# Sorted tokens of a mixture of experts: results added to x by accumulating indexed transfers, weights carried in the sorted rows

## The chip, the core and the metric

The kernel runs on one core of one Trainium2 chip. Its time is the device time of one execution in microseconds (us). The engines of the core work side by side, each through its own list of instructions: TensorE (PE in the profile, with its weight loads as PEld), VectorE (DVE), ScalarE (ACT), GpSimd (POOL), and SyncE (SP), which only issues transfers here. Transfers with an index per row (indexed transfers) are issued by GpSimd.

## The reference

The input x holds 8 batches of 1024 tokens of 128 numbers, in float32. Three layers follow one another:

```python
x = x + 0.5 * ffn(layernorm(x))     # layer 0
x = x + attention(layernorm(x))     # causal, one head, with rotary embedding
x = x + 0.5 * ffn(layernorm(x))     # layer 1, the same weights
```

The ffn is a mixture of 16 experts. A token's scores are `sigmoid(t @ gate_w.T)`; the four experts with the highest biased scores are chosen, and their scores, scaled to the sum 2.5, are the token's weights. An expert computes `silu(t @ g) * (t @ u)` with 64 units and multiplies by its down matrix. A shared expert is added for every token.

```python
for e in experts:
    y = y + weight[:, e] * (h_e(t) @ w2[e].T)     # weight is 0 for experts not chosen
y = y + h_shared(t) @ w2_shared.T
```

## The kernel before

A tile is 128 tokens, a group is 4 tiles (512 tokens), and a batch has 2 groups. Layer 0 of all batches and layer 1 of batches 4 to 7 are computed *dense*: every expert for every token. The experts are taken two at a time, in 8 pairs (class `Group`): a gate product (L651) and an up product (L657) of 512 columns on TensorE, the activation on ScalarE (L664), their product on VectorE (L668, "the units of a pair"), the weighing by the tokens' weights on GpSimd or VectorE (L673), and the down product (L684) that sums over pairs in PSUM. The weights are written to memory and spread from there over the partitions (L588, L597). One result per group is added to x on VectorE (L694) and, in layer 1, stored (L698).

Layer 1 of batches 0 to 3 is *sorted* (classes `SortedGroup`, `Chunk`, `Rows`), in two chunks of two batches. The router picks four experts per token. The chunk computes for each of its 16 tiles and each choice k the row at which the token stands when tokens are ordered by expert (`place`). The normalized tokens are scattered to these rows in memory by 64 indexed transfers of 128 rows (L1017). Blocks of 8 tiles of sorted rows are then loaded, transposed, and multiplied by the matrices of the expert that owns each tile (L1106, L1116, L1136); the results are copied from PSUM, one half of the block by ScalarE and the other by VectorE (L1143), and stored in `results`. At the end each tile of tokens gathers its four rows back, one indexed transfer for each k (L838). Meanwhile x with the shared expert's part has been kept in memory (`keep`, L817) and its buffer given back; it is fetched again (L834), VectorE adds each gathered row times its weight (L847), and the tile is stored (L854). The weight for each choice is looked up by three VectorE operations per group (L1003, L1009, L1013).

Attention (classes `Heads`, `Query`) lies between the layers, batch by batch.

The order of instructions on each engine is written by a planner when the program is built (class `Plan`). Every step has an engine, an assumed duration, a rank, the buffers that it takes and frees, and the steps that it waits for. The planner repeatedly picks the step that can begin first, and of those the one of lowest rank. A weighing may go to GpSimd or to VectorE, whichever can begin first (`instead`). After two indexed transfers in a row it puts a dummy operation of GpSimd, the pause (L247). So a change of a few steps can change the order of everything, and on the chip each engine keeps to the order as it was written.

Of the kernel before, what the change touches and what calls it, by code (L numbers as in the profile page):

```python
# [27 lines left out]
class Step:  # L28


    def __init__(self, engine, work, rank, emit, take, free, table, moves, indexed=False):
# [7 lines left out]
        self.left, self.next, self.ready, self.end = 0, [], 0.0, None  # L39


class Plan:
# [10 lines left out]
    def __init__(self, begin, pause):  # L53
        self.pause = pause
        self.in_row = 0
        self.steps = []
        self.places = {}
        self.held = {}
        self.free_at = dict.fromkeys(self.ENGINES, begin)
        self.transfers = begin  # L60
        self.table = None
# [9 lines left out]
    def add(self, engine, work, rank, emit, after=(), take=(), free=(), table=None, moves=0,  # L71
# [9 lines left out]
        return s  # L81

# [23 lines left out]
    def begin_of(self, s, t):  # L106
        t = max(t, s.ready)
        for pool in s.pools:
# [21 lines left out]
    def run(self):  # L130
# [12 lines left out]
        while todo:  # L143
# [29 lines left out]
            s.emit()  # L173
            todo -= 1
# [18 lines left out]
def kernel(  # L193
# [33 lines left out]
    LEAD = 8  # L227
# [25 lines left out]
    for name, n in {"gu": 3, "y": 1, "short": 3, "score": 2, "xs": 2}.items():  # L253
        plan.pool(name, n)
    buffers = {}
    for name, n, shape in (
        ("x", 9, [P, GT, D]),
        ("xn", 3, [P, GT, D]),
        ("xnc", CB * NG + 1, [P, GT, D]),
# [21 lines left out]
        ("combc", 1, [P, CT, E]),  # L281
        ("at", 1, [P, CT, E]),
        ("eq", 1, [P, GT, TOPK, E]),
        ("row", 4, [P, GT, D]),
        ("wt", 4, [P, GT, 2 * D]),
        ("got", 4, [P, TOPK + 1, D]),
        ("hs", 2, [P, W]),
    ):
        if not SORTED and name in ("xnc", "hTs", "chosen", "combc", "at", "eq", "row", "wt", "hs", "got"):
# [162 lines left out]
    def norm_steps(key, b, g, rank, after, tag, uses):  # L452
# [10 lines left out]
        def scale(j):  # L463
            nc.vector.tensor_scalar(
                buf(tag, n)[:, j, :], x_of(b, g)[:, j, :], mvs[n][:, j, 0:1], rstd[:, j : j + 1],
# [8 lines left out]
    def turn_steps(n, rank, after, tag, out_tag, uses):  # L474
# [3 lines left out]
        def turn():  # L478
            for j in range(GT):
                nc.tensor.transpose(tiles_of(bank_of(a))[:, j, :], buf(tag, n)[:, j, :], ident)  # L480
# [5 lines left out]
        return act(0.6, rank, copy, after=[s], free=end_short(a))  # L486
# [3 lines left out]
    class Group:  # L490
# [111 lines left out]
        def spread_steps(self, rank, after):  # L602
# [7 lines left out]
            return [  # L610
                sp(
                    1.0, rank, lambda h=h: self.load_weights(h), after=[s],
                    take=[("cb", (n, h), NP // 2)], moves=1.0,
                )
                for h in range(2)
            ]
# [86 lines left out]
        def expert_steps(self, p, last, hT, weights, shared):  # L703
# [5 lines left out]
            ready = []  # L709
            for k in range(NP):  # L710
# [3 lines left out]
                    0.86, rank, lambda k=k: self.gate(k), after=[hT, have_gate[w]],  # L714
                    take=[("pair", a, 1), ("gu", a, 1), ("sg", a, 1), ("hid", a, len(self.parts))],
                    free=[("hT", n)],
                )
                u = pe(
# [12 lines left out]
                ready.append(s)  # L731
            ends = []
# [31 lines left out]
        def steps(self, p, last, after):  # L764
# [4 lines left out]
            hT = turn_steps(n, rank, [s], "xn", "hT", 2 * NP + 2)  # L769
            shared = self.shared_steps(rank + 0.5, [hT])  # L770
            s = self.route_steps(rank, [hT])
            weights = self.spread_steps(rank, [s])
            return self.expert_steps(p, last, hT, weights, shared)
# [754 lines left out]
```

## Time and profile before

| | |
|---|---|
| median of 3 runs | 958.57 us (958.16 to 962.21) |
| profiled execution, own time | 960.61 us |
| its span, first to last instruction | 958.9 us |
| mean granted TensorE clock | 0.984 of full speed |
| instructions | 16331 |
| transfers | 136.93 MB, mean 143 GB/s |

The profile's page comes from one execution. "Busy" is the time in which an engine has an instruction at work. The slices cut the span into 40 parts of 24 us; each digit is the busy share in tenths. A group row names a line of the kernel, engine and operation, what it writes and reads with the shape, the count, then the busy time in us and the mean of one in ns, and then the idle time of the engine before them and what ended it. A timeline row gives the start in us, the duration in us, and the same names; a bracket at its end gives the idle time before it and the instruction that released it. In the trace a product of 512 columns is two matmul records[...].

### The profile page before, as it was taken

How to read it: one execution, taken by the hardware profiler on the slowest of the kernel's cores; microseconds unless marked ns; L12 is line 12 of the kernel's file. 1: busy time of each engine (PE TensorE's matmuls, PEld its weight loads, DVE VectorE, ACT ScalarE, POOL GpSimd, SP SyncE). 2: the span in 40 equal slices, each digit the busy share in tenths (PEclk: the TensorE clock that was granted, in tenths of full speed). 3: DMA queues.
4: the chain of work that ended last, by engine and by line, in shares of the span. 5: the costliest groups of instructions: out<-in, count | busy, mean ns of one | idle time of the engine just before them, and what ended most of it. 6: DMA issues, size and time to landing. Idle time of an engine off the chain costs nothing. (4 is left out here: it accounts for less than half of the span.)

```text
span 958.9 us, 16331 instructions
## 1 busy us (share of the span) xinstructions
PE 910.9 (95%) x5226; PEld 629.4 (66%) x5226; DVE 792.0 (83%) x2297; ACT 487.1 (51%) x818; POOL 657.3 (69%) x614
## 2 busy tenths in 40 slices
PE   9899999999998698999999999999999899999995
PEld 5556676666665475766676686776767766656663
DVE  7899878978888989889999866778888987777864
ACT  6336646558555324565565754566557464333220
POOL 2464615514488778988388988837877867888786
PEclk9899999999999899999999999999999999999998
DMA  5866327423132543134436887877598766566572
GB/s 167 201 181 175 77 69 209 119 49 89 45 110 57 126 122 88 50 82 110 117 104 179 219 215 212 228 189 196 147 254 196 197 192 147 136 159 145 135 170 53
DMA packets 147862, 136.93 MB, mean 143 GB/s; under 512 B 12160, under 2 KB 117440, under 8 KB 147648
## 3 DMA queue, kind: packets, MB, share of 16 engines
q1 hardware_dynamic: 138304, 117.83, 48.8%
q0 software_dynamic: 8192, 16.79, 6.3%
q10 hardware_dynamic: 1280, 1.26, 0.4%
q8 instruction: 41, 0.67, 0.3%
q14 instruction: 45, 0.37, 0.1%
HBM read 99.40 MB, written 36.44 MB: 142 GB/s over the span
## 5 line engine op out<-in xcount | busy, mean ns | idle before, releaser
L673 POOL TENSOR_TENSOR hid<-hid,cb 128x512 f32<-128x512 f32 x144 | 182.5, 1278 | 138.0 <-DVE hid L668 121.1
L684 PEld LDWEIGHTS psum<-wd,hid 128*128 128x128 f32 x1536 | 192.2, 195 | 34.2 <-issue 27.5
L684 PE MATMUL psum<-wd,hid 128*128 128x128 f32 x1536 | 202.9, 280 | 1.8 <-POOL hid L673 1.8
L657 PE MATMUL psum<-hT,wu 128*128 128x512 f32 x384 | 197.2, 595 | 3.5 <-DVE hid L668 3.5
L651 PE MATMUL psum<-hT,wg 128*128 128x512 f32 x384 | 198.2, 598 | 0.0
L664 ACT ACTIVATE sg<-psum 128x512 f32<-128x512 f32 x192 | 113.9, 598 | 156.9 <-PE psum L651 128.0
L668 DVE TENSOR_TENSOR hid<-psum,sg 128x512 f32<-128x512 f32 x192 | 131.2, 687 | 50.0 <-PE psum L657 33.1
L1017 POOL DMA_INDIRECT rows<-xnc,place x128 | 130.0, 1016 | 38.6 <-issue 29.5
L838 POOL DMA_INDIRECT got<-results,place x128 | 129.7, 1013 | 29.6 <-issue 28.3
L657 PEld LDWEIGHTS psum<-hT,wu 128*128 128x128 f32 x384 | 73.0, 191 | 96.9 <-issue 84.1
L1369 PEld LDWEIGHTS psum<-v,prT 128*128 128x128 f32 x576 | 71.0, 192 | 18.1 <-issue 13.1
L247 POOL TENSOR_TENSOR spare<-spare 128x4 f32<-128x4 f32 x76 | 80.5, 1060 | 1.7
L847 DVE SCALAR_TENSOR_TENSOR got<-got,wk 128x128 f32<-128x128 f32 x128 | 67.8, 544 | 14.3 <-DMA got<-results,place 13.3
L651 PEld LDWEIGHTS psum<-hT,wg 128*128 128x128 f32 x384 | 62.1, 192 | 25.4 <-issue 23.6
L1369 PE MATMUL psum<-v,prT 128*128 128x128 f32 x576 | 73.8, 276 | 1.8 <-ACT prT L1360 1.4
L1329 PE MATMUL psum<-k,q 128*128 128x512 f32 (+2 forms) x192 | 71.7, 497 | 2.6 <-DVE hid L668 2.4
L461 POOL TENSOR_TENSOR rs_f<-rs_f,neg_half 128x4 f32<-128x4 f32 x32 | 34.9, 1090 | 47.4 <-DVE rs_f L458 46.7
L443 DVE BATCH_NORM_STATS2 st<-x 128x6 f32<-128x128 f32 x192 | 53.4, 278 | 5.1 <-DMA x<-in_x 3.2
L1342 ACT ACTIVATE pr<-psum,top 128x128 f32<-128x128 f32 (+3 forms) x64 | 47.2, 740 | 17.5 <-DVE top L1339 12.5
L664 ACT ACT_TABLE_LOAD x38 | 48.8, 1283 | 8.3 <-PE psum L651 7.1
L1329 PEld LDWEIGHTS psum<-k,q 128*128 128x128 f32 x192 | 32.0, 195 | 28.3 <-issue 21.0
L1338 DVE TENSOR_REDUCE top<-psum 128x1 f32<-128x128 f32 (+3 forms) x64 | 48.4, 757 | 2.0
(143 smaller groups left out, 1505.2 us busy)
## 6 DMA issues: line engine op xcount, KB each, us to landing
cb<-cd SPq DMA_DIRECT2D x96, 512.0 KB
wt<-in_w_table SPq DMA_DIRECT2D x160, 128.0 KB
rows<-sums SPq DMA_DIRECT2D x20, 512.0 KB
row<-rows SPq DMA_DIRECT2D x40, 256.0 KB
results<-row SPq DMA_DIRECT2D x40, 256.0 KB
x<-in_x SPq DMA_DIRECT2D x16, 256.0 KB
kept<-x SPq DMA_DIRECT2D x8, 256.0 KB
rows<-xnc,place POOLq DMA_INDIRECT x128
```

What stands on the lines that cost most here:

```text
L247: nc.gpsimd.tensor_tensor(spare, spare, spare, ALU.pow)
L651: nc.tensor.matmul(pair_of(("gu", self.id, k))[0], wg[:, k * P : (k + 1) * P], self.hT(), start=True, stop=True,)
L657: nc.tensor.matmul(pair_of(("gu", self.id, k))[1], wu[:, k * P : (k + 1) * P], self.hT(), start=True, stop=True,)
L664: nc.scalar.activation(buf("sg", a), pair_of(a)[0], AF.Silu)
L668: nc.vector.tensor_tensor(buf("hid", a), pair_of(a)[1], buf("sg", a), ALU.mult)
L673: engine.tensor_tensor(hid, hid, cb, ALU.mult)
L684: nc.tensor.matmul(y[:, cols], units[:, cols], wsd if k == NP else wd[:, k, :], start=(self.terms[part] == 1 and j == tiles[0]), stop=(sel ...
L838: nc.gpsimd.indirect_dma_start(out=buf("got", (self.id, j))[:, k, :], out_offset=None, in_=self.chunk.results, in_offset=bass.IndirectOffs ...
L847: nc.vector.scalar_tensor_tensor(got[:, TOPK, :], got[:, k, :], self.chunk.weight[:, self.n * GT + j, k : k + 1], got[:, TOPK, :], ALU.mul ...
L1017: nc.gpsimd.indirect_dma_start(out=self.views[t * TOPK + k], out_offset=bass.IndirectOffsetOnAxis(ap=self.place[:, t, k : k + 1], axis=0), ...
L1329: nc.tensor.matmul(s[:, c:e], q[:, i * P : self.width], k[:, c:e], start=True, stop=True)
L1369: nc.tensor.matmul(o, buf("prT", self.id)[:, j, :], buf("v", self.b)[:, j, :], start=(j == 0), stop=(j == i),)
```

## The change

- The normalized tokens of a sorted group get 16 more columns, which hold the token's weights for the 16 experts, already halved (`R = D + E`, buffers `xnc`, rows in memory, loaded rows). They travel with the token in the scatter.
- After a block of sorted rows is loaded, VectorE finds each row's weight: it compares the owner of the row's tile (`own`) with the experts' numbers, multiplies by the 16 carried weights, and sums (`Rows.weights`). The results are multiplied by that weight as they leave PSUM (`result`): on ScalarE in four scalings of 128 columns, on VectorE in one product of 512.
- A gather adds its rows directly to x in SBUF (`compute_op=ALU.add`). The four additions of one tile wait for one another. They are ranked by k first, then by tile. After the last one the whole group is stored from x in one transfer.
- The lookup of weights per choice, the copy of x in memory, its fetch, VectorE's weighted addition, and the store by tiles are gone.
- x now stays in its buffer from loading until it is stored; there are 12 such buffers in place of 9.
- The planner gets `line`: a group's gate products and weight loads enter in the order in which groups were transposed. The gates of a group follow one another, as do its two weight loads, which also wait for the shared expert's step. The transposes of the second half of a query wait for those of the first.

```diff
--- before.py
+++ after.py
+    def line(self, name, key, enter, first, last):
+        self.lines[name] = []
+        enter.enters = (*enter.enters, (name, key))
+        for s in (first, last):
+            s.heads = name, key
+        last.leaves = True
...
         t = max(t, s.ready)
+        if s.heads and self.lines[s.heads[0]][:1] != [s.heads[1]]:
+            return float("inf")
...
             s.emit()
+            for name, key in s.enters:
+                self.lines[name].append(key)
+            if s.leaves:
+                self.lines[s.heads[0]].pop(0)
...
+    R = D + E
+    LEAD = 9
     SW = P // GT
...
-        ("x", 9, [P, GT, D]),
+        ("x", 12, [P, GT, D]),
         ("xn", 3, [P, GT, D]),
-        ("xnc", CB * NG + 1, [P, GT, D]),
+        ("xnc", CB * NG + 1, [P, GT, R]),
...
-        ("combc", 1, [P, CT, E]),
         ("at", 1, [P, CT, E]),
-        ("eq", 1, [P, GT, TOPK, E]),
-        ("row", 4, [P, GT, D]),
+        ("above", 1, [P, E, CT]),
+        ("row", 4, [P, GT, R]),
+        ("own", 2, [P, NS]),
+        ("part", 2, [P, GT, E]),
         ("wt", 4, [P, GT, 2 * D]),
-        ("got", 4, [P, TOPK + 1, D]),
         ("hs", 2, [P, W]),
     ):
...
+            loads = []
+            for h in range(2):
+                s = sp(
+                    1.0, rank, lambda h=h: self.load_weights(h), after=[s, shared],
                     take=[("cb", (n, h), NP // 2)], moves=1.0,
                 )
-                for h in range(2)
-            ]
...
-                    0.86, rank, lambda k=k: self.gate(k), after=[hT, have_gate[w]],
+                    0.86, rank, lambda k=k: self.gate(k),
+                    after=[hT, have_gate[w], *gates[-1:]],
                     take=[("pair", a, 1), ("gu", a, 1), ("sg", a, 1), ("hid", a, len(self.parts))],
                     free=[("hT", n)],
                 )
...
+            plan.line("gates", n, turned, gates[2], gates[-1])
...
-                buf("combc", self.chunk.n, "chunk")[:, self.tiles, :], self.sel, 0.5 * ROUTE_SCALE,
+                buf("xnc", self.id)[:, :, D:], self.sel, 0.5 * ROUTE_SCALE,
...
-        def keep(self):
-            nc.sync.dma_start(out=self.kept, in_=x_of(self.b, self.g))
...
-            s = dve(0.69, rank, self.shared_add, after=[s, normed], free=end_short(a))
-            self.away = sp(
-                0.5, rank, self.keep, after=[s], free=[("x", (self.b, self.g))], moves=0.25
-            )
+            self.summed = dve(0.69, rank, self.shared_add, after=[s, normed], free=end_short(a))
             return self.route_steps(rank, [hT])
-        def fetch(self, j):
-            nc.sync.dma_start(out=buf("got", (self.id, j))[:, TOPK, :], in_=self.kept[:, j, :])
         def gather(self, j, k):
             nc.gpsimd.indirect_dma_start(
-                out=buf("got", (self.id, j))[:, k, :], out_offset=None, in_=self.chunk.results,
+                out=x_of(self.b, self.g)[:, j, :], out_offset=None, in_=self.chunk.results,
                 in_offset=bass.IndirectOffsetOnAxis(
                     ap=self.chunk.place[:, self.n * GT + j, k : k + 1], axis=0
                 ),
-            )
-        def gathered(self, j, k):
-            got = buf("got", (self.id, j))
-            nc.vector.scalar_tensor_tensor(
-                got[:, TOPK, :], got[:, k, :], self.chunk.weight[:, self.n * GT + j, k : k + 1],
-                got[:, TOPK, :], ALU.mult, ALU.add,
-            )
-        def store_sorted(self, j):
-            t = self.g * GT + j
+                compute_op=ALU.add,
+            )
+        def store_sorted(self):
             nc.sync.dma_start(
-                out=in_tiles(out, self.b, slice(t, t + 1)),
-                in_=buf("got", (self.id, j))[:, TOPK : TOPK + 1, :],
+                out=in_tiles(out, self.b, tiles_of_group(self.g)), in_=x_of(self.b, self.g)
             )
         def gather_steps(self, rank, after):
+            ends = []
             for j in range(GT):
-                a = (self.id, j)
-                r = rank + 0.02 * j
-                before = [
-                    sp(
-                        0.5, r, lambda j=j: self.fetch(j), after=[*after, self.away],
-                        take=[("got", a, 1)], moves=0.064,
+                s = self.summed
+                for k in range(TOPK):
+                    s = pool(
+                        1.24, rank + k + 0.02 * (self.n * GT + j),
+                        lambda j=j, k=k: self.gather(j, k), after=[s, *after],
+                        moves=0.064, indexed=True,
                     )
-                ]
-                for k in range(TOPK):
-                    got = [
-                        pool(
-                            1.24, r, lambda j=j, k=k: self.gather(j, k),
-                            after=before if k == 0 else [*after, first], moves=0.064, indexed=True,
-                        )
-                    ]
-                    first = got[0] if k == 0 else first
-                    before = [
-                        dve(
-                            0.44, r, lambda j=j, k=k: self.gathered(j, k), after=[*got, *before]
-                        )
-                    ]
-                sp(
-                    0.5, r, lambda j=j: self.store_sorted(j), after=before, free=[("got", a)],
-                    moves=0.064,
-                )
+                ends.append(s)
+            sp(
+                0.5, rank, self.store_sorted, after=ends, free=[("x", (self.b, self.g))],
+                moves=0.25,
+            )
...
-            self.rows = dram.tile([NS * P, D], F32, name=f"rows{n}")
+            self.rows = dram.tile([NS * P, R], F32, name=f"rows{n}")
...
-        def weights(self, m, part):
...
+        def belongs(self):
+            nc.vector.tensor_copy(buf("own", self.n), bank_of(("op", self.n))[:, :NS])
...
+        def weights(self, h):
+            part = buf("part", (self.id, h))
+            q = 2 * self.i + h
+            shape = [P, GT, E]
+            nc.vector.tensor_tensor(
+                part, buf("own", self.chunk.n)[:, q * GT : (q + 1) * GT].unsqueeze(2).broadcast_to(shape),
+                counts[:, :E].unsqueeze(1).broadcast_to(shape), ALU.is_equal,
+            )
+            nc.vector.tensor_tensor(part, part, buf("row", (self.id, h))[:, :, D:], ALU.mult)
+            nc.vector.tensor_reduce(self.weight[h], part, AX.X, ALU.add)
         def result(self, h):
-            (nc.scalar.copy, nc.vector.tensor_copy)[h](
-                buf("row", ("y", self.id, h)), tiles_of(bank_of(("xd", self.id, h)))
-            )
+            y = tiles_of(bank_of(("xd", self.id, h)))
+            out = buf("row", ("y", self.id, h))
+            if h == 0:
+                for j in range(GT):
+                    nc.scalar.mul(out[:, j, :D], y[:, j, :], self.weight[h][:, j : j + 1])
+            else:
+                nc.vector.tensor_tensor(
+                    out[:, :, :D], y, self.weight[h].unsqueeze(2).broadcast_to([P, GT, D]), ALU.mult
+                )
...
+                weighed.append(
+                    dve(
+                        0.6, rank, lambda h=h: self.weights(h), after=[s, own],
+                        take=[("part", a, 1)],
+                        free=[("row", a), ("xs", a), ("part", a), ("own", self.chunk.n)],
+                    )
                 )
...
-                    (0.59, 0.69)[h], UNITS, lambda h=h: self.result(h), after=[s], free=end_short(b),
+                    (1.04, 0.69)[h], UNITS, lambda h=h: self.result(h), after=[s, weighed[h]], free=end_short(b),
...
```

## The prediction

> **What bounds the kernel now.** I read the page's shares and slices first, to see which engine is full and when.
>
> ```profile
> PE 910.9 (95%) x5226; PEld 629.4 (66%) x5226; DVE 792.0 (83%) x2297; ACT 487.1 (51%) x818; POOL 657.3 (69%) x614
> ...
> PE   9899999999998698999999999999999899999995
> ...
> DVE  7899878978888989889999866778888987777864
> ...
> POOL 2464615514488778988388988837877867888786
> ```
>
> TensorE is full nearly everywhere, so only what makes TensorE wait is worth time. VectorE is nearly as full in the first half; GpSimd fills up in the second.
>
> How much TensorE loses I took from the chain of waits and the timeline. Where it never waits a 512-column product takes 0.86 us, four 128-column products 0.89, four transposes 0.44. At these prices all its instructions sum to 876.8 us. Against that sum, its transposes of normalized tokens (L480) give a clock: one stands at 281.4 in the sum and at 304.1 in the trace (22.6 lost), others at 316.5 and 356.7 (40), 469.1 and 522.3 (53), 807.8 and 878.5 (71). TensorE ends at 949.7: 72.8 us lost, 54 of them before position 495, about 19 after.
>
> Why the first half loses I asked of VectorE's instructions, in their order, each at its mean from the groups. At the mark "units n done" (L668) the VectorE sum is ahead of TensorE's by 24.5 us at 281, 41.9 at 374, 50.1 at 459 and 51.8 at 492, close to the losses above; after that it falls to 7.5. So up to about 495 VectorE sets the pace. The timeline shows the sharpest case:
>
> ```profile
> 322.47 8.59 POOL L673 TENSOR_TENSOR hid<-hid,cb 128x512 f32<-128x512 f32 x7
> ...
> 323.62 7.52 DVE L790 TENSOR_TENSOR chosen<-rp,bi 128x64 f32<-128x64 f32 x1
> ...
> 332.55 0.45 PE L512 MATMUL psum<-ident,lt 128*128 128x128 f32 x1 [5.41 <-DVE x L1377]
> ```
>
> A small VectorE operation with two SBUF inputs (shortest of its line: 0.215 us) lasts as long as GpSimd's seven weighings in a row; TensorE then waits 5.4 us. Last, the tail:
>
> ```profile
> 949.05 0.61 PE L684 MATMUL psum<-wsd,sh 128*128 128x128 f32 x4
> 949.70 0.42 DVE L694 SCALAR_TENSOR_TENSOR x<-psum,x 128x256 f32<-128x256 f32 x1 [0.34 <-PE psum L684]
> ...
> 950.15 0.38 SPq L698 DMA_DIRECT2D out_x<-x  x1
> ...
> 953.30 1.01 POOL L838 DMA_INDIRECT got<-results,place  x1 [0.19 <-issue]
> ...
> 956.01 0.35 DVE L847 SCALAR_TENSOR_TENSOR got<-got,wk 128x128 f32<-128x128 f32 x1 [1.89 <-DMA got<-results,place]
> 956.39 0.33 SPq L854 DMA_DIRECT2D out_x<-got  x1
> ```
>
> TensorE is done at 949.7; gathers of the last tile, their additions and a store of 64 KB hold the end to 958.9.
>
> **The change, part by part.** Prices come from these rows (the last three stand for operations that the trace does not have):
>
> ```profile
> L673 POOL TENSOR_TENSOR hid<-hid,cb 128x512 f32<-128x512 f32 x144 | 182.5, 1278 | 138.0 <-DVE hid L668 121.1
> ...
> L838 POOL DMA_INDIRECT got<-results,place x128 | 129.7, 1013 | 29.6 <-issue 28.3
> ...
> L247 POOL TENSOR_TENSOR spare<-spare 128x4 f32<-128x4 f32 x76 | 80.5, 1060 | 1.7
> L847 DVE SCALAR_TENSOR_TENSOR got<-got,wk 128x128 f32<-128x128 f32 x128 | 67.8, 544 | 14.3 <-DMA got<-results,place 13.3
> ...
> L524 DVE TENSOR_TENSOR bi<-sc,gb 128x64 f32<-128x64 f32 x32 | 10.4, 325 | 1.1
> L544 DVE TENSOR_TENSOR sel<-sel,sc 128x64 f32<-128x64 f32 x24 | 10.4, 432 | 0.8
> ...
> L509 ACT COPY lt<-psum 128x128 f32<-128x128 f32 x32 | 8.5, 267 | 15.1 <-PE psum L503 14.2 <-PE psum L1106 0.7
> ```
>
> *VectorE.* Gone are 128 additions (67.8 us) and the look-up of weights (L1003, L1009, L1013: 4.3 + 7.4 + 3.3 = 15.0). New are, for each of 40 half blocks of sorted rows, a comparison, a product and a sum over 128x64: 0.325 + 0.432 + 0.216 (L548) = 0.97, 38.9 in all. The copy of half the results becomes a product of the same size (0.69 for 0.689: nothing). In the new order 13 more weighings fall to VectorE (48 to 61) at 0.748: 9.7. With 0.5 of small things: -33.7 us. Here a page of the Trainium skill speaks against the change: "SBUF — State Buffer", "Who interferes with whom", says that a VectorE operation with two SBUF inputs contends with GpSimd operations that read SBUF, and two of the three new ones are of that kind. If undisturbed they cost 0.22 + 0.23 + 0.22 (such operations in the timeline), 27 us in all; I keep the disturbed means, 38.9, and so does the rule.
>
> *Where that relief lies.* The additions went away from 650 us on, where TensorE was covered already; by itself that gains nothing. But the planner lays out everything anew, and its new order can be priced in the same manner: VectorE's lead is 27.5 us at position 247, 36 at 300, at most 41.7 at 421, then falls to -26. The peak is 51.8 - 41.7 = 10.1 us lower, and that I count on the path.
>
> *GpSimd.* 256 indexed transfers as before, 13 weighings fewer (-16.6), 12 pauses more (+12.7): -3.9. What an adding gather costs the trace doesn't show. Floor: the plain gather, 1.013; less is excluded, since it reads the same index and writes the same rows. Ceiling: reading the old value costs as much again, +1.013. I take 1.013: gather and scatter (1.016) differ in direction and not in price. The cover is thin: from position 504 the new order holds 367 us of GpSimd work (transfers with their 0.30 us of issue gap) against 373 of TensorE's and its 19 lost, so 25 us are free. The page "DMA: Bandwidth & Descriptors", "Rules for kernel authors", demands that an accumulating DMA wait for the earlier one on the same bytes. Its "Anatomy of one DMA" puts a transfer at 2.0 us + bytes / 436 GB/s, so by the rule four chained additions cost 4 x (1.31 + 2.15) = 13.8 us a tile. The row says otherwise: two transfers and a pause take 3.52 us, the new order puts 15 other gathers between two of the same tile, 16 x 1.76 = 28 us, and each has long landed. The rule costs one landing, at the end.
>
> *ScalarE.* 20 result copies of 0.587 become 80 scalings of 0.267: +9.6; table loads rise from 106 to 124 at 1.283: +23.1. It is busy 51%, so this is hidden behind TensorE; a bank held 0.5 us longer 20 times would cost 10 us if nothing covered it.
>
> *SP and the transfers.* 32 fetches, 8 keeps and 32 stores go, 8 larger stores come: 64 issues fewer. Rows grow from 512 to 576 bytes (29 MB become 33), the kept copies (4 MB) go: even. The queue is below 9 tenths in every slice. TensorE's own sum does not change.
>
> *Buffers.* Sorted batches now hold their x until their results are added: 8 of 12 buffers. Batches 6 and 7 are loaded only after batches 4 and 5 have been stored, and in the new order batch 7's attention ends about 60 us before TensorE does (before: 151). Its chain to the last group (normalize, route, spread weights, weigh) has a few us of slack where it had over a hundred. I count nothing, and keep it for a rival.
>
> *Tail.* Behind GpSimd's last weighing stand 13 gathers and 6 pauses, 6.5 x 3.52 = 23 us, against 31 us of TensorE work. So TensorE ends last: +0.49 to the store's issue (949.66 to 950.15 above), +3.0 for its landing (the 64 KB store took 2.5): 3.5 in place of 9.2.
>
> *Sum.* 876.8 + 41.7 + 3 (by which losses exceeded the lead at 459 and 492) + 18.8 (the second half's losses, unchanged) = 940.3; + 3.5 = 943.8 span. The profiled execution took 960.61 for a span of 958.9, so 945.5 in its terms, -15.1. The median of the runs is 2.0 below that execution: 943.5, say **944**.
>
> **The rivals.** A difference under 0.5%, here 953.8 to 963.4, can't be told from no change.
>
> *A (likeliest), 944*, own range 936 to 952: as above.
>
> *B, relief given back: 956.* Batch 7's chain runs late. Its spread weights stand in SP's queue behind the first store of sorted tokens, which waits for gathers, which wait behind four weighings on GpSimd. If two bursts like the 7.5 us one fall into this chain, 12 of the 15 us are gone. For: no cover. Against: the new order leaves slack at every hop.
>
> *C, slower: the adding gather is dear.* Each 0.1 us more adds 12.8 us to GpSimd; 25 us are free, then TensorE starves on weighings. It decides at (25 + 14.6) / 128 = 0.31 us above 1.013; at +0.5 the kernel takes 944 + 64 - 25 = 983. For: GpSimd is full in the second half, and the old value must be read. Against: both present directions cost the same.
>
> *D, more than expected: 933.* In the second half VectorE falls 34 us behind its former load; if this also ends half of the 19 us lost there, 944 - 10.
>
> *E, nothing but the tail: 953*, if the lead of VectorE isn't what starves TensorE. The agreement of leads and losses at four places speaks against it.
>
> **How the numbers follow.** A 0.45, B 0.16, C 0.22, D 0.09, E 0.08. Leaving out about half of D below and half of C above gives 933 to 975. Faster: A, D, some of E and a quarter of B, 0.62; within 0.5%: the most of B and the rest of E, 0.14; slower: C and the tail of B, 0.24.
>
> **What would show it.** Adding gathers near 1.01 us, the pair with its pause at 3.5; TensorE's last instruction near 940; losses near 45 us at position 500; the last event a store of x and no gather. It is wrong if the gathers take 1.3 us or more, if weighings on GpSimd end TensorE's waits, or if TensorE waits after 800 us for weights of the last groups.

## The result

The changed kernel takes 1019.43 us (median of 4 runs, 1019.28 to 1021.62) against 959.58 us of the kernel before in the same session (958.16 to 962.21): ratio 1.063, 95% interval 1.060 to 1.066. It is slower by 60 us, where the prediction had 944 and a range up to 975. The mechanism is that of rival C.

The shares, the slices and the software queue in the page of the changed kernel:

```profile
PE 930.5 (91%) x5226; PEld 642.6 (63%) x5226; DVE 791.5 (78%) x2280; ACT 521.0 (51%) x896; POOL 729.8 (72%) x613
...
PE   9899999999989899989997999997878998899788
...
DVE  6899889789988969897889677875547966776464
...
POOL 2464536146887878368889555999999759989996
...
q0 software_dynamic: 22528, 17.84, 9.8%
```

GpSimd stands at 9 in most slices from the 26th on, and TensorE has holes from the 28th on. GpSimd's busy time rose by 72.5 us, though it has 13 weighings fewer. The software queue moves 17.84 MB in 22528 packets; before it was 16.79 MB in 8192.

The groups of the changed kernel, costliest of each kind:

```profile
L693 POOL TENSOR_TENSOR hid<-hid,cb 128x512 f32<-128x512 f32 x131 | 176.2, 1420 | 120.2 <-DVE hid L688 95.7
L704 PE MATMUL psum<-wd,hid 128*128 128x128 f32 x1536 | 212.0, 287 | 40.5 <-POOL hid L693 36.2
...
L850 POOL DMA_INDIRECT x<-results,place x128 | 206.3, 1612 | 38.8 <-issue 29.2
...
L992 POOL DMA_INDIRECT rows<-xnc,place x128 | 129.5, 1011 | 29.9 <-issue 29.0
...
L264 POOL TENSOR_TENSOR spare<-spare 128x4 f32<-128x4 f32 x88 | 122.5, 1392 | 0.9
```

The adding gather (L850) takes 1612 ns where the plain one took 1013; the scatter (L992) is what it was. TensorE's down products (L704) now wait 36 us for weighings on GpSimd, against 1.8 us in the kernel before:

```profile
L684 PE MATMUL psum<-wd,hid 128*128 128x128 f32 x1536 | 202.9, 280 | 1.8 <-POOL hid L673 1.8
```

The pause (L264) and the weighing (L693) seem longer too, 1392 for 1060 and 1420 for 1278. Part of that is how records overlap, so I read the price from starts. In GpSimd's timeline of the kernel before, where only gathers stand, a pair of gathers and its pause repeat every 3.5 us:

```profile
925.14 0.95 POOL L838 DMA_INDIRECT got<-results,place  x1 [0.30 <-issue]
926.12 1.04 POOL L247 TENSOR_TENSOR spare<-spare 128x4 f32<-128x4 f32 x1
927.35 1.01 POOL L838 DMA_INDIRECT got<-results,place  x1 [0.19 <-issue]
928.66 0.95 POOL L838 DMA_INDIRECT got<-results,place  x1 [0.30 <-issue]
```

and in that of the changed kernel every 4.7 to 4.8 us (here from 651.10 to 655.80):

```profile
651.10 1.58 POOL L850 DMA_INDIRECT x<-results,place  x1 [0.16 <-issue]
652.99 1.56 POOL L850 DMA_INDIRECT x<-results,place  x1 [0.30 <-issue]
653.98 1.64 POOL L264 TENSOR_TENSOR spare<-spare 128x4 f32<-128x4 f32 x1
655.80 1.59 POOL L850 DMA_INDIRECT x<-results,place  x1 [0.19 <-issue]
```

The pause begins 0.57 us before the second gather's record ends. So the price is (4.75 - 3.52) / 2, about 0.62 us for each of 128 gathers: 79 us of GpSimd. In the waits between 632 and 1020 us this is the first row of TensorE:

```profile
PE psum L704 <- POOL hid L693: 36.0, 10, 7.5
```

(36.0 us in all, 10 times, 7.5 the longest). The tail in the timeline:

```profile
1011.61 1.70 POOL L850 DMA_INDIRECT x<-results,place  x1 [0.19 <-issue]
...
1016.01 0.61 PE L704 MATMUL psum<-wsd,sh 128*128 128x128 f32 x4
1016.66 0.42 DVE L714 SCALAR_TENSOR_TENSOR x<-psum,x 128x256 f32<-128x256 f32 x1 [3.60 <-PE psum L704]
1017.11 0.37 SPq L718 DMA_DIRECT2D out_x<-x  x1
```

TensorE ends last and a store of x follows it, as forecast.

Against the sum of TensorE's prices (876.8 us for both kernels) the losses, by the transposes of normalized tokens as before (L497 here), are:

| position in the sum, us | before, lost | changed, lost | forecast for changed |
|---|---|---|---|
| about 280 | 22.6 | 20.8 | |
| about 440 to 470 | 51 to 53 | 48.7 | |
| 487 (changed) | | 51.5 | |
| about 504 (changed), 515 (before) | 55.4 | 62.1 | 44.7 |
| about 600 | 57.8 | 68.0 | |
| about 760 | 69.7 | 111.0 | |
| TensorE's end | 72.8 | 139.8 | 63.5 |
| from there to the span's end | 9.2 | 3.3 | 3.5 |

Each column is one profiled execution, and these lie up to 4.4 us from the median of their kernel's runs, so two losses can differ by some 4 us by chance.

So there are two misses: 59 us behind position 504, where the gathers are, and 17 before it. The second has a visible case, in the timeline of VectorE, GpSimd and TensorE:

```profile
545.59 10.58 DVE L1119 TENSOR_TENSOR part<-part,row 128x64 f32<-128x64 f32 x1
546.28 2.50 POOL L1240 TENSOR_TENSOR sg<-sg,cs 128x512 f32<-128x512 f32 x2
548.73 1.27 POOL L1244 TENSOR_TENSOR q<-q,sg 128x512 f32<-128x512 f32 x1
549.96 1.26 POOL L1244 TENSOR_TENSOR k<-k,sg 128x512 f32<-128x512 f32 x1
551.17 4.91 POOL L693 TENSOR_TENSOR hid<-hid,cb 128x512 f32<-128x512 f32 x4
557.08 1.22 PE L677 MATMUL psum<-hT,wu 128*128 128x512 f32 x1 [7.07 <-DVE hid L688]
557.19 0.22 DVE L1119 TENSOR_TENSOR part<-part,row 128x64 f32<-128x64 f32 x1
```

The product of carried weights and mask, one of the change's new VectorE operations, takes 0.22 us in the median (last row). Here it stays 10.6 us, as long as GpSimd runs eight operations without a gap; VectorE's next product is late, and TensorE waits 7.1 us.

### The profile page after: what moved, and what is told of

Read it like the earlier page. It is cut to its first block, busy times and chain, and to the rows that moved or that the text cites. A ratio compares the mean times of both kernels' runs of the same rounds, so it can differ in the third digit from the quotient of the medians.

```text
span 1019.9 us, 16258 instructions
## 1 busy us (share of the span) xinstructions
PE 930.5 (91%) x5226; PEld 642.6 (63%) x5226; DVE 791.5 (78%) x2280; ACT 521.0 (51%) x896; POOL 729.8 (72%) x613
## 3 DMA queue, kind: packets, MB, share of 16 engines
q0 software_dynamic: 22528, 17.84, 9.8%
q10 hardware_dynamic: 1280, 1.26, 0.4%
## 4 chain that ended last, share of the span: by engine, by line
PE 52%; POOL 24%; DVE 16%; issue 6%; ACT 2%; DMA 0%; POOLq 0%; ACTq 0%; DVEq 0%
POOL x L850 15%; PE psum L704 12%; PE psum L671 9%; PE psum L677 9%; PE psum L1362 4%; POOL spare L264 4%; PE psum L1322 4%; POOL hid L693 3%; PE psum L1084 2%; PE psum L1349 2%; DVE hid L688 2%; PE psum L644 2%; DVE xn L481 2%; PE psum L497 1%; DVE top L1331 1%
## 5 line engine op out<-in xcount | busy, mean ns | idle before, releaser
L693 POOL TENSOR_TENSOR hid<-hid,cb 128x512 f32<-128x512 f32 x131 | 176.2, 1420 | 120.2 <-DVE hid L688 95.7
L704 PE MATMUL psum<-wd,hid 128*128 128x128 f32 x1536 | 212.0, 287 | 40.5 <-POOL hid L693 36.2
L704 PEld LDWEIGHTS psum<-wd,hid 128*128 128x128 f32 x1536 | 199.0, 202 | 71.6 <-POOL hid L693 42.4
L850 POOL DMA_INDIRECT x<-results,place x128 | 206.3, 1612 | 38.8 <-issue 29.2
L671 PE MATMUL psum<-hT,wg 128*128 128x512 f32 x384 | 200.6, 605 | 0.0
L992 POOL DMA_INDIRECT rows<-xnc,place x128 | 129.5, 1011 | 29.9 <-issue 29.0
L264 POOL TENSOR_TENSOR spare<-spare 128x4 f32<-128x4 f32 x88 | 122.5, 1392 | 0.9
L478 POOL TENSOR_TENSOR rs_f<-rs_f,neg_half 128x4 f32<-128x4 f32 x32 | 37.1, 1160 | 67.2 <-DVE rs_f L475 67.0
L671 PEld LDWEIGHTS psum<-hT,wg 128*128 128x128 f32 x384 | 63.2, 194 | 26.4 <-issue 24.4
L1335 ACT ACT_TABLE_LOAD x34 | 43.6, 1283 | 29.2 <-DVE top L1332 28.3
L693 DVE TENSOR_TENSOR hid<-hid,cb 128x512 f32<-128x512 f32 x61 | 57.0, 938 | 1.9 <-DMA cb<-cd 0.8
L481 DVE TENSOR_SCALAR xn<-x,mv_f,rs_f 128x128 f32<-128x128 f32 x96 | 48.7, 547 | 8.2 <-POOL rs_f L478 8.1
L1240 POOL TENSOR_TENSOR sg<-sg,cs 128x512 f32<-128x512 f32 x32 | 42.8, 1393 | 14.2 <-ACT sg L1230 8.8
```

Of the source, the lines that this page charges most:

```text
L264: nc.gpsimd.tensor_tensor(spare, spare, spare, ALU.pow)
L481: nc.vector.tensor_scalar(buf(tag, n)[:, j, :D], x_of(b, g)[:, j, :], mvs[n][:, j, 0:1], rstd[:, j : j + 1], ALU.subtract, ALU.mult,)
L671: nc.tensor.matmul(pair_of(("gu", self.id, k))[0], wg[:, k * P : (k + 1) * P], self.hT(), start=True, stop=True,)
L693: engine.tensor_tensor(hid, hid, cb, ALU.mult)
L704: nc.tensor.matmul(y[:, cols], units[:, cols], wsd if k == NP else wd[:, k, :], start=(self.terms[part] == 1 and j == tiles[0]), stop=(sel ...
L850: nc.gpsimd.indirect_dma_start(out=x_of(self.b, self.g)[:, j, :], out_offset=None, in_=self.chunk.results, in_offset=bass.IndirectOffsetOn ...
```

## Experiments

The kernel before takes 958.3 to 959.4 us (medians) beside these runs.

### Is it the adding, or the new order?

The changed kernel with plain gathers, order untouched:

```diff
-                compute_op=ALU.add,
```

> The changed kernel with its 128 gathers made plain: they write the rows over x in place of adding to it, so the addition of results to x is left out. Every instruction keeps its place. Theory (the adding gather is dear: 0.6 us more than a plain one, 128 times, of which 25 us were free): a gather takes 1.01 us again, a pair with its pause 3.5, and the time falls by 55 to 62 us, to 957 to 965. Rival (the new order is at fault: x held longer, batch 7's late chain, the last gathers ranked by k): the time stays above 1000 us. Second rival (half and half): about 985.

958.5 us, ratio to before 1.000 (0.999 to 1.002). That one argument costs 61 us. Its gathers, and TensorE's row of the waits between 632 and 1020 us:

```profile
L850 POOL DMA_INDIRECT x<-results,place x128 | 130.5, 1019 | 38.8 <-issue 28.4 <-DMA results<-row 9.3 <-DMA cb<-cd 0.2
```

```profile
PE psum L704 <- POOL hid L693: 0.5, 1, 0.5
```

The waits for weighings went from 36.0 to 0.5 us. TensorE's loss is still 62.7 us at position 504 and 81.1 at its end: 18.4 behind 504, where I had forecast 18.8. So x held longer, batch 7's late chain and the gathers ranked by k cost nothing that is seen. (This trace is of the slowest of 12 runs, 962.9 us.)

The other way round, the kernel before with adding gathers into its own buffers:

```diff
+    for g in buffers["got"]:
+        nc.gpsimd.memset(g, 0.0)
...
                     ap=self.chunk.place[:, self.n * GT + j, k : k + 1], axis=0
                 ),
+                compute_op=ALU.add,
             )
```

> The kernel before, with its 128 gathers made adding: they add to what stands in their buffer (set to 0 once at the start, then old rows), so the sums are not the reference's. Order and waits are those of before, VectorE's weighted additions stay. Theory (price of the adding gather): it takes 1.6 us and more, GpSimd has 80 us more to do in the second half, and the kernel takes 1015 to 1045 us. Rival (adding is slow only in the changed kernel, because its target x is in use by other engines or the four additions chase each other): a gather stays near 1.0 and the time within 5 us of before.

1015.05 us, ratio 1.057 (1.056 to 1.059).

```profile
L841 POOL DMA_INDIRECT got<-results,place x128 | 204.4, 1597 | 29.6 <-issue 28.6 <-DVE prT L1364 0.5
```

The same price in another order, with another target that no other engine uses meanwhile. It belongs to the transfer, and to nothing that the change put around it.

### What of the adding gather costs?

```diff
+            if self.chunk.n == 0:
                 nc.gpsimd.indirect_dma_start(
-                    out=x_of(self.b, self.g)[:, j, :], out_offset=None, in_=self.chunk.results,
+                    out=x_of(self.b, self.g)[:, j, :64], out_offset=None, in_=self.chunk.results,
...
+            else:
+                nc.gpsimd.indirect_dma_start(
+                    out=x_of(self.b, self.g)[:64, j, :], out_offset=None, in_=self.chunk.results,
+                    in_offset=bass.IndirectOffsetOnAxis(
+                        ap=self.chunk.place[:64, self.n * GT + j, k : k + 1], axis=0
+                    ),
...
-            self.results = dram.tile([NS * P, D], F32, name=f"results{n}")
+            self.res_d = 64 if n == 0 else D
+            self.results = dram.tile([NS * P, self.res_d], F32, name=f"results{n}")
...
-                in_=buf("row", ("y", self.id, h))[:, :, :D],
+                in_=buf("row", ("y", self.id, h))[:, :, : self.chunk.res_d],
```

> The changed kernel; the first chunk's 64 adding gathers bring only half of each row (64 columns, 256 B), the second chunk's 64 only half of the rows (64 partitions, 512 B each). Half of the additions to x is left out. Theory (the extra time is per row, since each row makes packets of its own): half-width gathers stay at 1.6 us, half-height ones take about 1.3. Rival (per byte): both about 1.3. Second rival (a fixed price of each adding transfer): both 1.6.

It ran once (1011.1 us), and only the gathers' own durations are read from it. Each line's in ns (least, median, most):

```profile
L851 POOL DMA_INDIRECT x<-results,place x64: 1542/1595/2122, 627.2 to 798.8; - x64
...
L859 POOL DMA_INDIRECT x<-results,place x64: 1411/1476/1973, 824.6 to 998.9; - x64
```

Half the bytes: 1595, against 1593 of the full gather. Half the rows: 1476, 0.12 less, where I had expected 1.3. So it is not the bytes, and only a small part goes with rows; the rival of a fixed price comes nearest. The software queue's packets, counted by size in the trace, tell what changes beside the price. A plain gather of the kernel before moves its 128 rows in 16 packets of 4096 B, with 16 of 4 B. An adding gather makes a packet of each row: 128 of 512 B, 128 of 256 B at half width, 64 of 512 B at half the rows, each time with 16 of 4 B. So 144 packets or 80 change the duration by 0.12 us, and the price does not go with the packets. Plain gathers of half the width or half the rows were not run, so how the extra 0.6 us itself splits stays open.

### Where did the relief of the first half go?

```diff
-            nc.vector.tensor_tensor(
-                part, buf("own", self.chunk.n)[:, q * GT : (q + 1) * GT].unsqueeze(2).broadcast_to(shape),
-                counts[:, :E].unsqueeze(1).broadcast_to(shape), ALU.is_equal,
-            )
-            nc.vector.tensor_tensor(part, part, buf("row", (self.id, h))[:, :, D:], ALU.mult)
-            nc.vector.tensor_reduce(self.weight[h], part, AX.X, ALU.add)
+            nc.vector.tensor_reduce(
+                self.weight[h], buf("row", (self.id, h))[:, :, D:], AX.X, ALU.add
+            )
```

> The changed kernel, in which a sorted row's weight is only the sum of the 16 carried numbers: the comparison and the product with two SBUF inputs are left out (weights are not the reference's), the reduction with one input stays. Theory (the missing relief of the first half is the product that stood 10.6 us behind GpSimd): no VectorE operation of this function lasts over 1 us, TensorE loses 8 to 11 us less before position 504, the rest is unchanged: 1008 to 1012 us. Rival (the next VectorE operation with two SBUF inputs takes the blow in its place): the same loss, 1017 to 1021 us. Either way the gathers keep their 1.6 us.

1010.4 us (1.054 of before, 1.052 to 1.056): 9.0 less than the changed kernel. TensorE's loss is 49.2 at position 487 and 52.5 at 504; it was 51.5 and 62.1. So 9.6 us are gone by position 504, 7.3 of them between 487 and 504, where the product had stood still; the rest is not told apart from the VectorE time that went with the two operations. The rival is there in part: at the same place another operation of two SBUF inputs was caught, for half as long, and TensorE lost 3 us instead of 10.

```profile
547.39 5.57 DVE L568 SCALAR_TENSOR_TENSOR comb<-sel,m 128x64 f32<-128x64 f32 x1
```

Both edits together:

> The changed kernel with both: plain gathers (results written over x) and a row's weight without the comparison and the product of two SBUF inputs. So the addition to x and the right weights are left out. Theory (the two causes are separate and add up): 1019 less 61 less 9, so 947 to 951 us, which is what the prediction made of the changed kernel with its two wrong terms taken out. Rival (with plain gathers the stuck product no longer matters, since GpSimd is the bound): 956 to 960.

952.8 us, ratio 0.9935 (0.991 to 0.996). The theory had 947 to 951, from the two effects added; the rival, in which the stuck product no longer matters, 956 to 960. It lies above the theory's range and below the rival's, 5.7 us under the run with plain gathers alone, where 9 were added up. TensorE's loss is 52.4 at position 504 and 68.5 at its end; the profiled span is 948.5.

### Does the pause matter?

The changed kernel without its 48 pauses between adding gathers:

```diff
-                    self.pause()
+                    if s.indexed != "add":
+                        self.pause()
```

> The changed kernel without the 48 pauses that stand between adding gathers (those between scatters stay); every other instruction keeps its place. Theory (GpSimd's total work in the second half is the bound, and a pause is part of it): a pause holds GpSimd about 1.0 us beside the gathers, so a pair with its pause falls from 4.8 to about 3.8 us, and the time by 40 to 50 us, to 970 to 980. Rival (the pause only fills time that the transfers need in any case): the gathers grow longer by as much, and the time stays at 1014 to 1024.

981.3 us, ratio 1.023 (1.020 to 1.026), just above the range; 38 us of the 60 come back. GpSimd's timeline:

```profile
631.04 1.54 POOL L851 DMA_INDIRECT x<-results,place  x1 [0.30 <-issue]
632.88 1.55 POOL L851 DMA_INDIRECT x<-results,place  x1 [0.30 <-issue]
634.74 1.54 POOL L851 DMA_INDIRECT x<-results,place  x1 [0.30 <-issue]
```

One adding gather every 1.85 us. The kernel before without the pauses between its plain gathers:

```diff
-                    self.pause()
+                    if s.indexed != "gather":
+                        self.pause()
```

> The kernel before, without the pauses between its plain gathers; every other instruction keeps its place. It tells whether 1.01 us is the whole price of a plain gather or whether the pause after each pair is a part of it. Theory (the pause is spare time): gathers stay at 1.0 us, a row of them runs at 1.25 us each, and the time is equal or up to 8 us shorter, 950 to 960. Rival (the pause gives the transfers time that they need): in a row without pauses the gathers take 1.5 us and more, or hold GpSimd between them, and the time is 960 or more.

952.3 us, ratio 0.993 (0.991 to 0.996): 0.7% below the kernel before.

```profile
692.32 0.95 POOL L839 DMA_INDIRECT got<-results,place  x1 [0.30 <-issue]
693.57 0.95 POOL L839 DMA_INDIRECT got<-results,place  x1 [0.30 <-issue]
694.83 0.95 POOL L839 DMA_INDIRECT got<-results,place  x1 [0.30 <-issue]
```

1.25 us each, without pauses. This is the clean pair of numbers: 1.85 against 1.25, so adding costs 0.60 us of GpSimd a transfer. And in these kernels the pause only spent time. With no pause between scatters either, in the new order that the planner then writes:

```diff
-    IN_ROW, PAUSE = 2, 1.05
+    IN_ROW, PAUSE = 1000000, 1.05
```

> The kernel before without any pause, between scatters and between gathers, in the order that its planner writes when it counts none. Computes the reference in full. Theory (a pause is only spent time, for plain transfers of either direction): scatters and gathers stay at 1.0 us, 79 us of GpSimd work are gone, and the time is below that of the run without pauses between gathers alone: 940 to 950 us. Rival (scatters need their pauses, or VectorE sets the pace in the first half whatever GpSimd does): 950 to 956 us.

956.3 us, ratio 0.997 (0.996 to 0.999), above both ranges. Scatters take 988 ns, so they need no pause here, but the gain over leaving the order alone did not come; GpSimd has 44 us less to do than there, and that bought nothing. The trace tells where it was lost. Behind position 525 TensorE loses 11 us, as much as in the run before this one, but up to there it has lost 9 us more. There VectorE and TensorE have these rows:

```profile
523.14 6.07 DVE L541 TENSOR_TENSOR sel<-rp,bi 128x64 f32<-128x64 f32 x1
531.36 1.62 PE L624 MATMUL psum<-hT,ws 128*128 128x512 f32 x2 [3.02 <-DVE hs L1127]
```

Again a small operation with two SBUF inputs stands still, here while GpSimd runs five weighings in a row (522.98 to 529.12), and TensorE waits for what comes behind it. How much of the 9 us it accounts for was not separated.

### Can the planner make up for it?

The price told, pauses kept:

```diff
-                        1.24, rank + k + 0.02 * (self.n * GT + j),
+                        1.88, rank + k + 0.02 * (self.n * GT + j),
```

> The changed kernel, whose planner is told 1.88 us for an adding gather in place of 1.24; the program computes the same, in a new order. Theory (GpSimd's total from the first gather on is the bound): weighings move from GpSimd to VectorE, which has 24 us less to do there than before; some of the 59 us come back, 990 to 1010 us. Rival (the gathers' own length sets the end whatever the order): within 5 us of the changed kernel, 1014 to 1024 us.

1004.9 us, ratio 1.047 (1.045 to 1.049). TensorE now ends at 958.9 of a span of 1003.8: five weighings more went to VectorE and TensorE starves no more, but the gathers run on alone for 45 us. So what ends last is GpSimd's own work. The price told as 1.86 (the same line), and no pause between adding gathers, which the planner knows:

```diff
-                if not s.indexed or t - self.free_at[e] > self.PAUSE:
+                if s.indexed in (False, "add") or t - self.free_at[e] > self.PAUSE:
...
-                self.in_row += s.indexed
+                self.in_row += s.indexed is True
```

> The changed kernel with adding gathers, no pause between them, and a planner that is told 1.86 us for each and no pause. Computes the reference in full. Theory (the two gains seen one by one, 38 us without pauses and 15 with the price told, add up in part, since both shorten the same wait for weighings): 958 to 970 us. Rival (telling the price gains nothing once the pauses are gone): 978 to 984.

968.0 us, ratio 1.008 (1.006 to 1.011), as expected: even so the adding gather leaves the kernel 0.8% above the one before, and 1.6% above the one before without pauses between its gathers (952.3).

### The rest of the change, without adding gathers

Weights carried in the rows, results weighed as they leave PSUM, plain gathers into a buffer of five rows (the fifth the kept x), one sum:

```diff
-                out=x_of(self.b, self.g)[:, j, :], out_offset=None, in_=self.chunk.results,
+                out=buf("got", (self.id, j))[:, k, :], out_offset=None, in_=self.chunk.results,
...
-                compute_op=ALU.add,
...
+        def gathered(self, j):
+            got = buf("got", (self.id, j))
+            nc.vector.tensor_reduce(buf("sum", (self.id, j)), got.rearrange("p k d -> p d k"), AX.X, ALU.add)
```

> The change with weights carried in the rows, but with plain gathers into a buffer of five rows (four results and the kept x, as before the change), which VectorE sums in one reduction with one input, 32 in place of 128 additions; x has 9 buffers again. Computes the reference in full. Theory (plain gathers give back the 60 us, and 32 reductions at about 0.75 us lie where VectorE is covered): 948 to 962 us. Rival (the freed VectorE time was needed for weighings there): 970 us and more.

1011.8 us, ratio 1.055 (1.052 to 1.057): a miss by 50, and not by the rival's reason. TensorE's last product and the last gathers:

```profile
946.47 0.61 PE L706 MATMUL psum<-wsd,sh 128*128 128x128 f32 x4
...
999.28 0.95 POOL L855 DMA_INDIRECT got<-results,place  x1 [0.30 <-issue]
999.65 1.23 DVE L871 TENSOR_REDUCE sum<-got 128x128 f32<-128x640 f32 x1 [4.81 <-DMA got<-results,place]
1000.54 0.95 POOL L855 DMA_INDIRECT got<-results,place  x1 [0.30 <-issue]
...
1005.61 1.23 DVE L871 TENSOR_REDUCE sum<-got 128x128 f32<-128x640 f32 x1 [4.73 <-DMA got<-results,place]
```

TensorE ends at 947.1. There are only two buffers for gathered rows; each is held through fetch, four gathers, landing and sum, and so the last tiles pass one every 6 us. With four buffers (one each of `part` and `sum` in place of two), the fetch behind the first gather and an urgent sum:

```diff
-        ("x", 9, [P, GT, D]),
+        ("x", 7, [P, GT, D]),
...
-        ("got", 2, [P, TOPK + 1, D]),
+        ("got", 4, [P, TOPK + 1, D]),
...
-                    0.5, r, lambda j=j: self.fetch(j), after=[*after, self.away],
+                    sp(0.5, UNITS, lambda j=j: self.fetch(j), after=[got[0], self.away], moves=0.064)
```

> As the run with plain gathers into a buffer of five rows, but with four such buffers in place of two (x has 7, the half-block weights 1), the fetch of x ordered after a tile's first gather, and the reduction ranked as urgent. Computes the reference in full. Theory (what cost 50 us there was only that a tile's buffer comes free after its landing and its reduction, so that two buffers let the gathers run on 65 us after TensorE): the gathers end with TensorE, 950 to 958 us, a little better than before the change. Rival (32 reductions and plain gathers are themselves too much beside the weighings): 965 and more.

962.6 us, ratio 1.004 (1.003 to 1.005). TensorE now ends last (at 959.6, its store follows), so the time for which buffers were held was the cause; which of the three edits did it was not separated. The time is 5 us above what I expected. The reduction over 640 numbers, read with a stride, takes 1.26 us and not the 0.75 that I had set for it, and VectorE is busy 85%. The trace has a larger item, in the first half:

```profile
495.17 9.38 DVE L1139 TENSOR_TENSOR part<-own,counts 128x64 f32<-128x64 f32 x1
506.10 1.47 PE L499 MATMUL psum<-ident,xn 128*128 128x128 f32 x4 [5.72 <-DVE xn L483]
```

The comparison of one half block, the other new operation with two SBUF inputs, stands still while GpSimd runs eight operations (494.65 to 504.47), and TensorE waits 5.7 us for the normalization behind it. Up to position 452 TensorE had lost some 11 us less than in the kernel before, about the relief that was forecast; by 482 it has lost 9.7 us more. What the kernel takes without that stall no run shows. The change without its adding gathers is no gain in this form.

## Why the prediction was wrong

**What bounds the kernel: right.** TensorE's sum (876.8) and its losses closed on both kernels, and each number below is a difference of such losses.

**The failed step: "I take 1.013: gather and scatter (1.016) differ in direction and not in price."** The adding gather costs 0.60 to 0.62 us more. The floor was taken because a plain transfer of either direction cost the same; but direction says nothing of the accumulating mode, which no row of the trace had. The bounds were right (0 to 1.013 above), the value was set at the cheap end. With the middle of the bounds, 0.5, my own formula gave 983; with the measured 0.62 it gives 944 + 79 - 25 = 998.

**"25 us are free": near.** 128 x 0.62 = 79 us more of GpSimd's work made TensorE lose 59 us more than forecast behind position 504, so 20 were covered, 5 fewer than I had and little more than such losses differ by chance. The chance of C, 0.22, was too low for an operation of unknown price on an engine with so thin a cover: the decision point, 0.31, stood well inside my own bounds.

**"The peak is 51.8 - 41.7 = 10.1 us lower, and that I count on the path": failed.** At 504 the loss is 62.1 where 44.7 was forecast: 17.4 us more. 9.6 of these go when the two operations of two SBUF inputs are left out. I had charged the three new operations at disturbed mean prices, and the sum was near (43.9 us for 38.9). But a sum spreads over 40 places what falls on one: a single one of 10.6 us at a spot where TensorE waited. The run with four buffers shows the same in another order, 9.4 us at one comparison. What the Trainium skill's "SBUF — State Buffer", "Who interferes with whom", says of such operations I used as a price; it should have been read as a chance of a long stall. The other 8 us are not settled by a run. VectorE's timeline has three more operations stuck for 5.4, 5.5 and 4.7 us in this stretch (L558, L812, L568), and the losses grow by 8.1 and 8.7 us next to the first two; that they are the cause is argued, not shown.

**VectorE's "-33.7 us": failed.** Its busy time fell by 0.5 us (792.0 to 791.5), and by 13.7 with plain gathers (778.3). The means of the kernel before did not hold in the new order: the 61 weighings on VectorE took 938 ns each where I had set 748 (57.0 us for 45.6), and the 64 normalizations before attention 699 for 476 (L481, 41.7 us for 27.0 of the kernel before). What this cost TensorE was not separated.

**Second half "18.8, unchanged": right without the adding** (18.4 with plain gathers, one execution). **Chained additions, one landing in all: right.** The 38.8 us for which GpSimd idles before adding gathers are 29.2 of issue, 9.3 of one wait for results and 0.3 for VectorE; none is a wait for an earlier gather. The 13.8 us a tile was an estimate for additions that follow one another directly. **Tail: right**, 3.3 for 3.5. **ScalarE, SP, buffers at nothing: nothing speaks against it**; they are in the run with plain gathers too, whose second half came out as forecast.

**The rivals.** C was right, at 0.62 above. B's burst did happen, once, and not in the late chain for which it was put forward, but in the first half. D did not come: with plain gathers and without the stuck product the second half loses 16.1 us and not the 9 that D had; behind 632 us VectorE is busy 10 us less than in the kernel before (243 against 253, with plain gathers) and not 34.

With the price at 0.62 and the first half as it was, the sum is 943.8 + 79 - 25 + 17.4 = 1015 for the span, against 1019.9. The last 5 us are those by which the cover came out at 20 and not 25; the lower granted clock (below) lies there too, and no run separates it.

## What to carry to other kernels

An operation in a mode that the trace does not show (here: accumulating) should not be given the price of its plain form; measure it, or forecast from the middle of its bounds, above all where it sits on an engine with little cover. Work moved off one engine onto an indexed transfer is paid by the engine that issues the transfer: here 68 us of VectorE additions, most of them covered, were traded for 79 us of GpSimd, of which TensorE paid 59. And a short VectorE operation costs its mean only where something covers its longest case.

## What was not expected

- An adding gather's duration does not depend on the row's width (1595 ns at 256 B, 1593 at 512 B) and little on the number of rows (1476 at 64 rows), and each of its rows is a packet of its own, where plain gathers put eight in one.
- A small VectorE operation can stand still through eight GpSimd operations in a row (10.6 us for one of 0.22 us), not only through one. It is not only those with two tensors as inputs: the normalization of one tensor (L481, TENSOR_SCALAR) took 6.15 us at 770.32 in the changed kernel, against 0.5 in the mean, while GpSimd ran operation on operation.
- The pauses between indexed transfers bought nothing: plain ones ran at 1.25 us each, adding ones at 1.85, in rows of five and more.
- Starving TensorE also made its products longer. Of the 58.8 us between the spans of the changed kernel and its run with plain gathers, 42.8 are idle time of TensorE and 16.0 busy time (930.5 against 914.5), at a granted clock of 0.965 against 0.982. From 700 to 760 us it was 0.89 against 1.00, and behind 630 us the longest gate product (L671) took 1061 ns against 697, with a median of 592 and 593. The clock records of the two traces have only two values, full and half: up to the end of TensorE's work it is at half for 44 us behind 630 us in the changed kernel, and for 3.4 us with plain gathers, in stretches of 3.4 or 6.8 us. "TensorE: Matmul & The Clock Gate" of the Trainium skill, "Part 1: The HAM clock gate", says that the clock falls to half after an idle window of about 3.4 us; the waits for weighings here reach 7.5 us, and the two agree.
